# Two state-space layers on one core: the old sum added on VectorE at the copy-out, and u * D made by ScalarE

## The chip, the cores and the metric

The kernel runs on one core of a Trainium2 chip. The metric is the device time of one execution in microseconds; three runs of the kernel before are at hand. In the text, PE is TensorE's matrix unit and PEld its loading of weights, DVE is VectorE, ACT is ScalarE, POOL is GpSimd, and SP is SyncE, whose queue issues nearly all DMAs. PSUM is the memory that TensorE writes, SBUF the memory that everything else works in.

## The reference

Four images of 64 x 64 positions with 192 channels pass through two layers, each added to its own input. Cut to what matters, with D_INNER = 384 channels and 16 states:

```python
# layer 0: four directions k over the 4096 positions, each with its own weights
h = dA * h + dBu                       # 16 states per channel, along the positions
y_k = einsum("bkdn,bkn->bkd", h, ct)   # sum over the states
out_k = y_k + u * Ds                   # skip term
y = out_0 + flip(out_2) + transpose(out_1) + transpose(flip(out_3))
# then LayerNorm over the channels, times silu(z), and a projection back to 192

# layer 1: the same four directions over a 3 x 3 depthwise convolution,
# all with the same weights
xc = silu(conv(x_val) + conv_b)
y = y1 + y2 + y3 + y4                  # each one: scan(u) + u * D_param
```

The skip term of the second layer is the same for all four directions, so their sum is 4 * D * u.

## The kernel before

**First layer.** `FirstLayer.run` goes through the four images (batches) one after the other: `between` finishes one batch and projects the next, then `scans` does the recurrences. The sum y lives in DRAM as 4096 x 384. `project_steps` writes u times the sum of the D's into it, and every piece of scan adds to it.

`scans` cuts a batch into 32 items. An item is one direction k and one chunk c of 512 positions; directions 0 and 2 (by row) come first, then 1 and 3 (by column), 16 items each. Every item has 16 states, and one state is one step of the loop over g; n is the state's number in its item. For each state, ACT makes the decays (`decay`, L728) and the product with B (`b_product`, L716), PE turns the product from positions on partitions to channels on partitions (`turn_x`, L733), DVE scans three blocks of 128 channels (`scan`, L741, with a small reduction L751 that keeps the last column), POOL multiplies by C (`c_product`, L755), and PE turns the result back while it adds it into three PSUM banks (`add_y`, L768). The additions lag by LAG = 3 states. At state 3 there are therefore none; at state 4 those of two states are done, and later one state per step.

The order on PE, DVE, ACT and POOL is written out by hand: each engine executes its instructions in the order in which the loop emits them. `Item.steps` lists the preparation of the next items with their places (dt through `dt_rows` L632, `absolute` L638 on ACT, `delta` L661 on DVE and so on), and `prepare` puts them into the loop. The DMAs on SP are ordered by a scheduler and wait in their queue for buffers; those of the C rows (`bct`, L721, one for two states, three buffers) wait for POOL.

Old y enters an item in PSUM: `load` brings the chunk of y to SBUF as `yold` (L601, one buffer), `start_y` (L762) multiplies the identity by it on PE at states 3 and 4 with the flag that opens the accumulation, and `add_y` adds on top. When the item is complete, `end_y` (L781) copies the banks to SBUF on DVE during states 2 and 3 of the next item, and a DMA (L784) stores them. The load for the next item is issued at state 5, except where the direction changes from row to column: there the chunk of y is spread over all that was stored before, and the load comes after the last `end_y` of the item before:

```python
if n == 5 and i + 1 < len(items) and items[i + 1].k % 2 == it.k % 2:
    q = items[i + 1]
    q.yold = load("yold", self.y_dram, q.k, q.c)
```

**Second layer.** `SecondLayer.project` goes through the four batches. For each of three channel blocks e, ACT writes the padded image (`pad`, L1123), and for each half q of the image ACT starts the convolution with tap 0 (`acc`, L1135) and DVE adds the eight others (L1137). ACT makes u from it with Silu (L1138), copies the border rows and columns that the scans need (L1145, L1148), and PE multiplies each block of 128 positions of u by `dg`, a diagonal matrix with 4 * D, which turns it and scales it at once (L1155). ACT copies the result out (L1159) and SP stores it as the first content of y. `acc` and `u` have three buffers each, `dq` two banks. The order of this stage is set by a scheduler. `prepare`, `scans` and `finish` follow.

Of the kernel before, what the change touches and what calls it, by code (L numbers as in the profile page):

```python
# [10 lines left out]
F32 = mybir.dt.float32  # L11
AF = mybir.ActivationFunctionType
# [4 lines left out]
DI, NS, DR, KD = 384, 16, 12, 4  # L17
ND = DI // 128
CB, NC2 = 96, 2
LC = 512  # L20
# [382 lines left out]
class FirstLayer:  # L403
# [168 lines left out]
    def scans(self):  # L572
        nc, tc = self.tc.nc, self.tc
        with ExitStack() as ctx:
# [3 lines left out]
            ps_y = pool("psy", 1, space=bass.MemoryType.PSUM)  # L578
            ps_x = pool("psx", 3, space=bass.MemoryType.PSUM)
            ps_m = pool("psm", 2, space=bass.MemoryType.PSUM)  # L580
            ident = self.ident
# [16 lines left out]
            def load(name, dram, k, c):  # L598
                t = p1.tile([128, NJ, DI], F32, name=name)
                for to, of in rows(t, dram, k, c):  # L600
                    nc.sync.dma_start(to, of)  # L601
                return t
# [100 lines left out]
            items = []  # L703
# [4 lines left out]
            flat = [(it, n) for it in items for n in range(NS)]  # L708
# [45 lines left out]
                it, n = flat[g]  # L754
                nc.gpsimd.tensor_tensor(hs[g], hs[g], bc(cs[g - n % 2][:, n % 2, :], 1, ND), ALU.mult)  # L755

            def start_y(it, b):

                if b == 0:
                    it.yp = [ps_y.tile([128, LC], F32, name=f"yp{i}") for i in range(ND)]  # L760
                yo = it.yold.rearrange("p j e -> p (j e)")[:, b * LC : (b + 1) * LC]
                nc.tensor.matmul(it.yp[b], ident, yo, start=True, stop=False, skip_group_check=True)  # L762

            def add_y(g, b):
                it, n = flat[g]
                for i in range(NJ):
                    j, d = divmod(b * NJ + i, ND)
                    nc.tensor.matmul(  # L768
                        it.yp[b][:, i * 128 : (i + 1) * 128],
                        hs[g][:, d, j * 128 : (j + 1) * 128],  # L770
                        ident,
                        start=False,
                        stop=n == NS - 1,
                        is_transpose=True,
                        skip_group_check=True,
                    )

            def end_y(it, b):
                if b == 0:
                    it.yt = p1.tile([128, NJ, DI], F32, name="yt")  # L780
                nc.vector.tensor_copy(it.yt.rearrange("p j e -> p (j e)")[:, b * LC : (b + 1) * LC], it.yp[b])  # L781
                if b == ND - 1:
                    for of, to in rows(it.yt, self.y_dram, it.k, it.c):
                        nc.sync.dma_start(to, of)  # L784
# [3 lines left out]
            def gate_in(t, e):  # L788
                zs[t, e] = self.in_proj(ps_m.tile([128, LC], F32, name="zp", tag="m"), ND + e, t)
# [8 lines left out]
            with tc.manual_schedule(engines={nc.tensor.engine, nc.scalar.engine, nc.vector.engine, nc.gpsimd.engine}):  # L798
                tc.keep_in_program_order(nc.scalar.preload_act_table_set("natural_log_exp_and_others"))
                plan = {}  # L800
                for i, it in enumerate(items):
                    for ahead, n, engine, f in it.steps():
                        if i < ahead:
                            f()
                        else:
                            plan.setdefault((i - ahead) * NS + n, []).append((engine, f))
                for t in range(NCH):
                    for e in range(ND):
                        plan.setdefault(t * NS + 13 + e, []).append(("pe", lambda t=t, e=e: gate_in(t, e)))
                        plan.setdefault(t * NS + 15 + e, []).append(("act", lambda t=t, e=e: gate_out(t, e)))  # L810

                def prepare(g, engine):
                    for e, f in plan.get(g, []):
                        if e == engine:
                            f()

                items[0].yold = load("yold", self.y_dram, items[0].k, items[0].c)
                c_rows(0)
                b_product(0)
                b_product(1)  # L820
                decay(0)
                for d in range(ND):
                    turn_x(0, d)
                LAG = 3
                late = []
                for g in range(N + LAG + 1):
                    i, n = divmod(g, NS)
                    it = items[i] if g < N else None
                    before = items[i - 1] if i > 0 else None
                    prepare(g, "act")  # L830
                    if g + 2 < N:
                        if g % 2 == 0:
                            c_rows(g + 2)
                        b_product(g + 2)
                    if g + 1 < N:
                        decay(g + 1)
                    adds = [[] for _ in range(ND)]
                    if it is not None:
                        for at, b in (((LAG, 1), 0), ((LAG, 2), 1), ((LAG + 1, 0), 2)):
                            if at[0] == n:  # L840
                                adds[at[1]].append((start_y, it, b))

                    ready = [x for x in late if x <= g - LAG and (n > LAG or x // NS < i)][:2]
                    for j, (x, b) in enumerate((x, b) for x in ready for b in range(ND)):
                        adds[j // len(ready)].append((add_y, x, b))
                    late = [x for x in late if x not in ready]
                    for d in range(ND):
                        if g < N:
                            scan(g, d)
                        if d == 1:  # L850
                            prepare(g, "dve")
                        if before is not None and (n, d) in ((LAG - 1, 2), (LAG, 0), (LAG, 1)):
                            end_y(before, {2: 0, 0: 1, 1: 2}[d])
                            if (n, d) == (LAG, 1) and it is not None and it.yold is None:
                                it.yold = load("yold", self.y_dram, it.k, it.c)
                        if g + 1 < N:
                            turn_x(g + 1, d)
                        for f, *a in adds[d]:
                            f(*a)
                    if g < N:  # L860
                        prepare(g, "pe")
                        c_product(g)
                        late.append(g)
                        prepare(g, "pool")
                        if n == 5 and i + 1 < len(items) and items[i + 1].k % 2 == it.k % 2:
                            q = items[i + 1]
                            q.yold = load("yold", self.y_dram, q.k, q.c)


    def finish(self, batches):  # L870
# [152 lines left out]
class SecondLayer(FirstLayer):  # L1023
# [6 lines left out]
    def __init__(self, tc, ctx, consts, w, dram, alive):  # L1030
        nc = tc.nc
        self.tc, self.w, self.alive, self.dram = tc, w, alive, dram
        self.ident, self.group, self.one = consts
        wp = ctx.enter_context(tc.tile_pool(name="ws", bufs=1))
# [30 lines left out]
        nc.vector.memset(self.keep, 1.0)  # L1065
        for at in (0, SEG, 3 * SEG - 1, 4 * SEG - 1):
            nc.vector.memset(self.keep[:, at : at + 1], 0.0)

        self.dg = wp.tile([128, ND, 128], F32, name="dg_s")
        d = load("D", [128, 1, ND])  # L1070
        nc.vector.tensor_scalar_mul(d, d, float(KD))
        for e in range(ND):
            nc.vector.tensor_scalar_mul(self.dg[:, e, :], self.ident, d[:, 0, e : e + 1])

    def run(self, batches):

# [11 lines left out]
    def project(self, batches):  # L1088
        nc, tc = self.tc.nc, self.tc
        with ExitStack() as ctx:  # L1090
# [17 lines left out]
            for b, (_, y, gate, uc_dram) in enumerate(batches):  # L1108
# [7 lines left out]
                for e in range(ND):  # L1116
# [12 lines left out]
                    for q in range(2):  # L1129
                        nh = half * rows  # L1130
                        acc = pa.tile([128, nh, HW], F32, name="acc")
                        part = lambda tap: pad[:, q * nh + tap // 3 : q * nh + tap // 3 + nh, tap % 3 : tap % 3 + HW]
                        weight = lambda tap: self.cw[:, e, tap : tap + 1]
                        u = pu.tile([128, nh, HW], F32, name="u")
# [6 lines left out]
                        n = SEG // HW  # L1141
# [5 lines left out]
                                to = uc[:, r, e, k * SEG : (k + 1) * SEG].rearrange("p (w h) -> p w h", h=HW)  # L1147
                                nc.scalar.copy(to[:, :, q * nh : (q + 1) * nh], wide[:, col : col + n, :])  # L1148

                        flat = u.rearrange("p h w -> p (h w)")  # L1150
                        for t in range(half):
                            dq = pq.tile([128, NJ, 128], F32, name="dq")
                            for j in range(NJ):
                                at = t * LC + j * 128
                                nc.tensor.matmul(  # L1155
                                    dq[:, j, :], flat[:, at : at + 128], self.dg[:, e, :], start=True, stop=True
                                )
                            du = pl.tile([128, NJ, 128], F32, name="du")
                            nc.scalar.copy(du, dq)  # L1159
                            at = (q * half + t) * LC  # L1160
                            to = y[at : at + LC, e * 128 : (e + 1) * 128].rearrange("(j p) e -> p j e", p=128)
                            nc.sync.dma_start(to, du)
# [470 lines left out]
```

## Time and profile before

| what | us |
|---|---|
| median of 3 runs | 11105.2 |
| lowest and highest run | 11085.83 and 11113.26 |
| the profiled execution | 11106.54 |
| its span, first to last instruction | 11104.6 |
| PE busy in the span | 9551.9 (86%) |
| DVE busy | 9693.3 (87%) |
| ACT busy | 9775.8 (88%) |
| POOL busy | 8587.9 (77%) |

The first layer takes the first 9670 us or so, the second the rest: its projection lies roughly between 9750 and 10330 us. The granted TensorE clock is 0.939 of full speed over the span, and the trace has it in stretches of full and of half speed. A busy share is a mean over stages with different limits, so the question for each part of the change is which wait ends last in its own stage. The profile counts one f32 matmul of this kind as two records and one f32 transpose as one, so "x768" for L762 is 384 matmuls, three for each of the 128 items.

### The profile page before, as it was taken

Reading aid. Unit: us, or ns where it says so; the run is one execution under the profiler, and the core shown is the slowest. Engines: PE = TensorE matmul, PEld = TensorE weight load, DVE = VectorE, ACT = ScalarE, POOL = GpSimd, SP = SyncE. Lnnn points to the kernel's source line nnn. Section 1 sums busy time; section 2 is a strip of 40 time slices with the busy share of each in tenths; the row PEclk is TensorE's granted clock in tenths of the full one; section 3 lists DMA queues with packets and bytes.
Section 4 is the critical chain, followed back from the end, with each engine's and each line's share of the span. In section 5 each row is a group of like instructions: output and inputs, shape, how many; then the busy total and the mean of one; then the engine's idle time right before and its main releaser. Section 6 shows DMA issues by size and latency. Waiting matters only on the chain. (4 is left out here: it accounts for less than half of the span.)

```text
span 11104.6 us, 172135 instructions
## 1 busy us (share of the span) xinstructions
PE 9551.9 (86%) x61449; PEld 7273.6 (66%) x61449; DVE 9693.3 (87%) x11515; ACT 9775.8 (88%) x16979; POOL 8587.9 (77%) x2776
## 2 busy tenths in 40 slices
PE   7998888888988888888988888889988888788677
PEld 4776666666776666656776666657766766655366
DVE  4999899976999899968999899949998999878675
ACT  5999999977999999969999999959999999856477
POOL 3999899955999899938999899929998999700370
PEclk8999999998999999998999999989999999989688
DMA  4333344344333344443333433353333434433458
GB/s 125 109 108 101 91 101 101 98 137 127 109 106 101 92 101 99 98 159 112 109 103 96 98 97 99 93 168 109 109 99 95 98 98 98 120 119 123 157 131 272
DMA packets 833671, 1267.54 MB, mean 114 GB/s; under 512 B 102026, under 2 KB 517655, under 8 KB 832292
## 3 DMA queue, kind: packets, MB, share of 16 engines
q1 hardware_dynamic: 827940, 1250.15, 40.5%
q0 software_dynamic: 4864, 6.29, 0.4%
q8 instruction: 488, 8.00, 0.3%
q14 instruction: 379, 3.10, 0.1%
HBM read 955.83 MB, written 300.42 MB: 113 GB/s over the span
## 5 line engine op out<-in xcount | busy, mean ns | idle before, releaser
L755 POOL TENSOR_TENSOR h<-h,bct 128x1536 f32<-128x1536 f32 x2048 | 7062.9, 3470 | 579.9 <-DVE carry L751 477.5
L741 DVE TENSOR_TENSOR_SCAN h<-a,carry,x 128x512 f32<-128x512 f32 x5376 | 6604.9, 1266 | 231.0 <-PE x L733 194.9
L733 PE MATMUL x<-ident,xT 128*128 128x128 f32 x24576 | 4000.8, 287 | 811.8 <-DVE h L741 710.1
L716 ACT ACTIVATE xT<-dtuT,bT 128x384 f32<-128x384 f32 x8192 | 4358.8, 609 | 93.0 <-PE x L733 87.3
L733 PEld LDWEIGHTS x<-ident,xT 128*128 128x128 f32 x24576 | 2804.0, 145 | 2136.5 <-DVE h L741 920.5
L728 ACT ACTIVATE a<-dt,A_log_f 128x512 f32<-128x512 f32 x6144 | 3977.7, 716 | 0.0
L768 PE MATMUL yp<-ident,h 128*128 128x128 f32 x24576 | 3703.1, 277 | 9.2 <-POOL h L755 9.2
L768 PEld LDWEIGHTS yp<-ident,h 128*128 128x128 f32 x24576 | 2944.2, 144 | 78.8 <-issue 62.6
L632 PE MATMUL dp<-xd,w_dtb_f 13*128 13x512 f32 x1536 | 882.7, 657 | 216.0 <-DVE dt L661 211.3
L741 DVE TENSOR_TENSOR_SCAN h<-a,x 128x512 f32<-128x512 f32 x768 | 899.1, 1207 | 191.3 <-PE x L733 114.0
L645 POOL TENSOR_SCALAR wl<-e 128x1536 f32<-128x1536 f32 x128 | 189.2, 1478 | 799.3 <-ACT e L641 406.2
L519 PE MATMUL pp<-xT,w_in 96*128 96x512 f32 x1152 | 539.2, 617 | 1.1 <-DVE xw L562 1.1
L632 PEld LDWEIGHTS dp<-xd,w_dtb_f 13*128 13x128 f32 x1536 | 235.0, 189 | 456.6 <-DVE dt L661 341.3
L762 PE MATMUL yp<-yold,ident 128*128 128x512 f32 x768 | 445.1, 664 | 72.7 <-DMA yold<-y 72.7
L1137 DVE SCALAR_TENSOR_TENSOR acc<-pad,conv_w_s,acc 128x2048 f32<-128x2048 f32 x192 | 439.3, 2342 | 53.5 <-ACT acc L1135 52.9
L638 ACT ACTIVATE e<-dp 128x512 f32<-128x512 f32 x384 | 224.7, 585 | 269.3 <-DVE dt L661 155.4
L1118 POOL MEMSET pad<- 128x66 f32 x12 | 1.9, 158 | 578.4 <-DVE acc L1137 458.9
L658 POOL TENSOR_TENSOR e<-e,wl 128x1536 f32<-128x1536 f32 x128 | 445.1, 3477 | 0.3
L655 POOL TENSOR_TENSOR e<-e,dt 128x1536 f32<-128x1536 f32 x128 | 442.9, 3460 | 0.3
L751 DVE TENSOR_REDUCE carry<-h 128x3 f32<-128x3 f32 x2048 | 322.7, 158 | 70.4
L519 PEld LDWEIGHTS pp<-xT,w_in 96*128 96x128 f32 x1152 | 221.3, 198 | 244.4 <-issue 234.3
L661 DVE SCALAR_TENSOR_TENSOR dt<-dp,e 128x512 f32<-128x512 f32 x384 | 255.5, 666 | 65.2 <-POOL e L658 58.7
(170 smaller groups left out, 6875.3 us busy)
## 6 DMA issues: line engine op xcount, KB each, us to landing
bct<-xp SPq DMA_DIRECT2D x1024, 512.0 KB, 4.9
uT<-uT SPq DMA_DIRECT2D x64, 768.0 KB, 4.7
yold<-y SPq DMA_DIRECT2D x64, 768.0 KB, 7.9
y<-yt SPq DMA_DIRECT2D x64, 768.0 KB, 4.5
uT<-uT SPq DMA_DIRECT2D x128, 384.0 KB, 5.0
yold<-y SPq DMA_DIRECT2D x128, 384.0 KB, 5.3
y<-yt SPq DMA_DIRECT2D x128, 384.0 KB, 4.6
zg<-gate SPq DMA_DIRECT2D x64, 768.0 KB, 6.3
```

The source lines that it names most:

```text
L519: self.tc.nc.tensor.matmul(pp, self.w_in[:, i, e * 128 : (e + 1) * 128], self.xT[:, i, t * LC : (t + 1) * LC], start=(i == 0), stop=(i == ...
L632: nc.tensor.matmul(self.dp[d], w, self.xd[0 : DR + 1, :], start=True, stop=True)
L655: nc.gpsimd.tensor_tensor(self.e, self.e, self.dt, ALU.subtract)
L658: nc.gpsimd.tensor_tensor(self.e, self.e, self.wl, ALU.add)
L716: nc.scalar.mul(xTs[g][:, j, :], it.dtuT[:, j * DI : (j + 1) * DI], it.bT[:, j, n : n + 1])
L728: nc.scalar.activation(as_[g][:, d, :], it.dt[:, d, :], AF.Exp, scale=scale)
L733: nc.tensor.transpose(xs[g, d][:, j * 128 : (j + 1) * 128], xTs[g][:, j, d * 128 : (d + 1) * 128], ident)
L741: nc.vector.tensor_tensor_scan(along(hs[g][:, d, :], it.k), along(as_[g][:, d, :], it.k), along(xs.pop((g, d)), it.k), 0.0 if it.first els ...
L755: nc.gpsimd.tensor_tensor(hs[g], hs[g], bc(cs[g - n % 2][:, n % 2, :], 1, ND), ALU.mult)
L762: nc.tensor.matmul(it.yp[b], ident, yo, start=True, stop=False, skip_group_check=True)
L768: nc.tensor.matmul(it.yp[b][:, i * 128 : (i + 1) * 128], hs[g][:, d, j * 128 : (j + 1) * 128], ident, start=False, stop=n == NS - 1, is_tr ...
L1137: nc.vector.scalar_tensor_tensor(acc, part(tap), weight(tap), acc, ALU.mult, ALU.add)
```

## The change

In the first layer, `start_y` goes. The first addition of an item opens each bank (`start` at n == 0 and i == 0), and `end_y` adds old y on DVE while it copies from PSUM. Every item now loads its own `yold` at state 8, the turn of directions included. In the second layer ACT writes 4 * D * u over `acc` in one instruction for each half image, with D as the scale per partition, and PE turns it with a plain transpose. The matrix `dg` is no longer built.

```diff
-            def start_y(it, b):
-
-                if b == 0:
-                    it.yp = [ps_y.tile([128, LC], F32, name=f"yp{i}") for i in range(ND)]
-                yo = it.yold.rearrange("p j e -> p (j e)")[:, b * LC : (b + 1) * LC]
-                nc.tensor.matmul(it.yp[b], ident, yo, start=True, stop=False, skip_group_check=True)
-
             def add_y(g, b):
                 it, n = flat[g]
+                if n == 0 and b == 0:
+                    it.yp = [ps_y.tile([128, LC], F32, name=f"yp{i}") for i in range(ND)]
                 for i in range(NJ):
...
-                        start=False,
+                        start=n == 0 and i == 0,
...
             def end_y(it, b):
                 if b == 0:
                     it.yt = p1.tile([128, NJ, DI], F32, name="yt")
-                nc.vector.tensor_copy(it.yt.rearrange("p j e -> p (j e)")[:, b * LC : (b + 1) * LC], it.yp[b])
+                part = slice(b * LC, (b + 1) * LC)
+                yt, yo = (t.rearrange("p j e -> p (j e)")[:, part] for t in (it.yt, it.yold))
+                nc.vector.tensor_add(yt, it.yp[b], yo)
...
-                items[0].yold = load("yold", self.y_dram, items[0].k, items[0].c)
...
-                    if it is not None:
-                        for at, b in (((LAG, 1), 0), ((LAG, 2), 1), ((LAG + 1, 0), 2)):
-                            if at[0] == n:
-                                adds[at[1]].append((start_y, it, b))
...
-                            if (n, d) == (LAG, 1) and it is not None and it.yold is None:
-                                it.yold = load("yold", self.y_dram, it.k, it.c)
...
-                        if n == 5 and i + 1 < len(items) and items[i + 1].k % 2 == it.k % 2:
-                            q = items[i + 1]
-                            q.yold = load("yold", self.y_dram, q.k, q.c)
+                        if n == 8:
+                            it.yold = load("yold", self.y_dram, it.k, it.c)
...
-        self.dg = wp.tile([128, ND, 128], F32, name="dg_s")
         d = load("D", [128, 1, ND])
-        nc.vector.tensor_scalar_mul(d, d, float(KD))
-        for e in range(ND):
-            nc.vector.tensor_scalar_mul(self.dg[:, e, :], self.ident, d[:, 0, e : e + 1])
+        self.d4 = wp.tile([128, ND], F32, name="d4_s")
+        nc.vector.tensor_scalar_mul(self.d4, d[:, 0, :], float(KD))
...
-                        flat = u.rearrange("p h w -> p (h w)")
+                        nc.scalar.activation(acc, u, AF.Identity, scale=self.d4[:, e : e + 1])
+                        flat = acc.rearrange("p h w -> p (h w)")
...
-                                nc.tensor.matmul(
-                                    dq[:, j, :], flat[:, at : at + 128], self.dg[:, e, :], start=True, stop=True
-                                )
+                                nc.tensor.transpose(dq[:, j, :], flat[:, at : at + 128], self.ident)
```

## The prediction

> **What bounds the kernel now.** I read the page first, for what is busy. These are its rows of the first layer's scans; a row gives busy time and mean ns of one instruction, then idle time just before it and what ended most of that.
>
> ```profile
> L755 POOL TENSOR_TENSOR h<-h,bct 128x1536 f32<-128x1536 f32 x2048 | 7062.9, 3470 | 579.9 <-DVE carry L751 477.5
> L741 DVE TENSOR_TENSOR_SCAN h<-a,carry,x 128x512 f32<-128x512 f32 x5376 | 6604.9, 1266 | 231.0 <-PE x L733 194.9
> L716 ACT ACTIVATE xT<-dtuT,bT 128x384 f32<-128x384 f32 x8192 | 4358.8, 609 | 93.0 <-PE x L733 87.3
> L762 PE MATMUL yp<-yold,ident 128*128 128x512 f32 x768 | 445.1, 664 | 72.7 <-DMA yold<-y 72.7
> ```
>
> The scans of one batch last about 2195 us (first to last L751), four times. In the stretch 700 to 1100 us ACT is busy 389.2 of 400 us, DVE 382.9, POOL 375.7, PE 352.3. Three engines are nearly full, and PE, from which the change takes most, is the loosest. So the 445 us of L762 are not 445 us of time; what counts is where PE makes the others wait. The view of waits names one such place:
>
> ```profile
> PE yp L762 <- DMA yold<-y: 72.7, 4, 18.4
> ```
>
> Four waits of 18 us, one per batch. The timeline at 1316 us (start, length, idle before) shows that everything stands still there:
>
> ```profile
> 1317.03 2.07 PE L762 MATMUL yp<-yold,ident 128*128 128x512 f32 x2 [18.07 <-DMA yold<-y]
> ...
> 1320.05 2.13 ACT L716 ACTIVATE xT<-dtuT,bT 128x384 f32<-128x384 f32 x4 [15.95 <-PE x L733]
> 1320.06 1.22 DVE L741 TENSOR_TENSOR_SCAN h<-a,x 128x512 f32<-128x512 f32 x1 [17.70 <-PE x L733]
> ...
> 1321.61 3.45 POOL L755 TENSOR_TENSOR h<-h,bct 128x1536 f32<-128x1536 f32 x1 [14.62 <-ACT xT L716]
> ```
>
> This is item 17 of 32, the first of the column direction. Its load of old y must wait until the item before has stored, and start_y on PE waits for the load, with turn_x for DVE queued behind. From the ends of L751 (one per state) I took the length of each item: most lie between 67.1 and 71.4 us, item 17 of the four batches is 86.2, 84.8, 84.7 and 84.9.
>
> Splitting DVE's idle time by state: from state 12 of one item to state 8 of the next it waits for almost nothing (0.03 us a state, 0.2 us at states 3 and 5). Its waits are at states 9 to 11, when ACT has itself stood 1.4 us at Abs (L638) for DVE's delta. So in a common item neither the matmuls of L762 nor their place hold anybody, and their removal gives little directly.
>
> One exception is PE's clock. At state 3 nothing is to be added to y, and PE has only the turns and start_y. In stretches of 3.4 us around 1726 us (busy time and count of PE, PEld, DVE, ACT, POOL, then PEclk):
>
> ```profile
> 1722.40:1725.80 3.40, 1.24 (x11) 0.82 (x9) 3.40 (x5) 3.40 (x7) 3.40 (x2) 1.00 0.22 72
> 1725.80:1729.20 3.40, 3.40 (x11) 2.04 (x10) 3.37 (x5) 3.40 (x7) 3.40 (x2) 0.50 0.89 197
> 1729.20:1732.60 3.40, 3.40 (x22) 2.38 (x21) 3.10 (x4) 3.40 (x7) 3.40 (x2) 1.00 0.40 119
> ```
>
> A stretch with 1.24 us of PE work is followed by one at half clock. There start_y takes longer and pushes a turn back, and DVE waits (timeline):
>
> ```profile
> 1726.14 1.91 PE L762 MATMUL yp<-yold,ident 128*128 128x512 f32 x2
> ...
> 1732.00 0.60 PE L733 MATMUL x<-ident,xT 128*128 128x128 f32 x4
> ...
> 1732.70 2.59 DVE L741 TENSOR_TENSOR_SCAN h<-a,carry,x 128x512 f32<-128x512 f32 x2 [0.38 <-PE x L733]
> ```
>
> The clock in the trace halves in this way from state 3 in 34 of 128 items. There state 5 takes 4.39 us instead of 3.77, and in the first eight items of a batch state 3 takes 0.6 us more too.
>
> [...]
>
> **The change, part by part.** The groups for the replaced operations:
>
> ```profile
> L681 DVE TENSOR_TENSOR dtuT<-tp,uT 128x512 f32<-128x512 f32 x384 | 259.0, 674 | 18.8 <-PE tp L675 8.7
> L781 DVE COPY yt<-yp 128x512 f32<-128x512 f32 x384 | 258.2, 674 | 17.7 <-PE yp L768 17.4 <-issue 0.3
> L1155 PE MATMUL dq<-dg_s,u 128*128 128x128 f32 x768 | 115.1, 315 | 52.0 <-ACT u L1138 50.7 <-ACT du L1159 1.3
> L1135 ACT ACTIVATE acc<-pad,conv_w_s 128x2048 f32<-128x2048 f32 x24 | 48.3, 2013 | 0.6
> ```
>
> 1. end_y: 384 copies from PSUM become 384 adds of PSUM and SBUF. L681 is that shape, under the same load: 674 ns against 674. Cost 0.
>
> 2. Turn of direction: the load is issued at state 8 of its own item and first used ten states (some 40 us) later, in end_y. The store it must wait for was issued at state 3. SP still waits for that store's landing (4.6 us) ahead of the load's issue, as before, with bct loads queued behind it; POOL has two pairs of states in hand (14 us), so nobody is reached. Item 17 falls from 85.2 (mean) to 68.3: 16.9 x 4 = **-68**. The usual loads also lose SP's wait for PE (186.9 us in SP's view of waits), on no path: SP waits 6953 us for POOL anyway.
>
> 3. L762 gone, 384 matmuls of 1.16 us on PE. Directly: DVE's 34 slips at state 5 go, 34 x 0.62 = 21, and some 0.6 x 8 at state 3: **-26**.
>
> 4. The gap at state 3. Without start_y, PE has some 6.5 us with only 16 turns (12 in 5.3 us), so each item holds a window like the one at 1722.4, wherever it falls. Half clock then reaches into state 4, where PE has 24 additions and 12 turns to do, 4.0 us at full clock (0.44 us for four) and 7.8 at half (0.87), against DVE's 3.77. By hand, in that order (turn, 8 adds, three times): half clock for the first 3.2 us makes DVE wait 0; for 4.3 us 0.5; for 6 us 1.2. How far it reaches depends on the window's phase and on whether the second window is also too empty (it would hold 8 to 15 turns and adds; windows below about 12 are followed by half clock nearly always in this trace, fuller ones seldom). Over the phases I get 0.4 us an item; bounds 0 (a start before state 4) and 1.3 (two full windows). Take 0.4 x 124 = **+50**.
>
> 5. Second layer: 24 more ACTIVATEs at 2.01 us, 48 us on ACT, which from 9900 to 10340 us is busy 59%, beside the convolution (L1137) that DVE runs without gaps, 192 x 2.34. acc is now held until turned, some 8 us longer; its next writer is needed two convolutions (37 us) later, so that cover holds. In the order after, tap 0 comes behind the new ACTIVATE and up to three du copies, still well inside. It counts where batches meet and at the end (DVE idles 14 us between batches): +2.0, and the turns save: 16 matmuls go from two passes to one, some 2 us at each. Four places of 0 to 1: **+2**, between -6 and +10. The removed setup of dg is 0.7 us beside other work. DMA count and bytes do not change.
>
> Sum: -68 - 26 + 50 + 2 = -42. The profiled execution took 11106.5 (span 11104.6), 1.3 above the median of 11105.2; so **11064**.
>
> **Rivals.** A: half clock costs nothing, as start_y's own 1.9 us was what hurt. For it: the shown item slips because of start_y. Against: windows get emptier. 11064 - 50 = 11014. B, slower: the gap makes two half-clock windows in each item; at 1.3 us, 161 - 94 + 2 = +69, 11174. It decides from 1.0 us per item, where the sum is 33 above the present time. For it: PE is already full at states 4 to 8. C: the stall at item 17 moves, say to end_y because the load in two pieces queues badly: +68 on the sum, 11132. Against: ten states of slack. D: the 48 us of ACT in the second layer come on the path, 11110; against, 41% idle. E: the steady gain of 2 and 3 only in part, as ACT's 97% takes over: that lies in my range.
>
> **How the numbers follow.** Chances: the sum above 0.58 (own range 11026 to 11113, for 0.1 to 0.8 us an item), A 0.17, B 0.10, C 0.08, D 0.07. A difference of 0.3%, 33 us, is about what a measurement of this kernel tells from none. Faster by more: A, and two thirds of the first case: 0.57. Within: the rest of it, D and half of C: 0.30. Slower: B and part of C: 0.13. The range 11005 to 11125 leaves out B, much of C and the edge of A.
>
> **What would show it.** Right: no wait at item 17 (all items 67 to 71 us); end_y's add at 670 to 680 ns; PEclk of 0.5 from state 3 in nearly every item, and state 5 longer by some 0.4; second layer's projection unchanged within 10 us. Wrong: state 5 at 3.77 in all items (A) or above 4.8 (B), a wait of end_y for yold (C), or DVE gaps between convolutions (D).

## The result, and the profile after

The changed kernel took **11067.1 us** (median of 15 runs, 11053.0 to 11079.5), the kernel before 11101.3 beside it (15 runs, 11084.4 to 11113.4). The ratio is 0.9971, with a 95% interval of 0.9964 to 0.9978: faster by about 0.3%, 34 us. The profiled execution took 11062.1 (span 11060.3), 44.4 less than that of before; the granted clock of TensorE over the span went from 0.939 to 0.918.

The groups of the scans after; the columns are those of before. The additions into yp now stand at L763, end_y at L778.

```profile
L755 POOL TENSOR_TENSOR h<-h,bct 128x1536 f32<-128x1536 f32 x2048 | 7066.0, 3473 | 550.0 <-DVE carry L751 508.2
L741 DVE TENSOR_TENSOR_SCAN h<-a,carry,x 128x512 f32<-128x512 f32 x5376 | 6615.6, 1267 | 274.7 <-PE x L733 224.1
...
L716 ACT ACTIVATE xT<-dtuT,bT 128x384 f32<-128x384 f32 x8192 | 4358.2, 609 | 34.7 <-PE x L733 29.7
...
L763 PE MATMUL yp<-ident,h 128*128 128x128 f32 x24576 | 3839.9, 285 | 9.2 <-POOL h L755 9.2
```

Before, the additions stood so:

```profile
L768 PE MATMUL yp<-ident,h 128*128 128x128 f32 x24576 | 3703.1, 277 | 9.2 <-POOL h L755 9.2
```

POOL, DVE and ACT do the same work at the same price; the additions, the same in number and shape, have become dearer for PE. DVE's idle time ahead of these scans has grown from 231.0 to 274.7 us, 224.1 of it waiting for turned products (L733), while ACT's idle time ahead of its products has fallen from 93.0 to 34.7: one wait has gone and another has grown. The row of the multiplications by the identity has gone, and the view of waits has no line of PE waiting for yold.

The operations that the change put in, and the taps of the convolution beside them:

```profile
L1123 DVE SCALAR_TENSOR_TENSOR acc<-pad,conv_w_s,acc 128x2048 f32<-128x2048 f32 x192 | 440.6, 2342 | 46.2 <-ACT acc L1121 44.9
...
L778 DVE TENSOR_TENSOR yt<-yp,yold 128x512 f32<-128x512 f32 x384 | 258.4, 674 | 20.9 <-PE yp L763 17.4 <-issue 0.7
...
L1142 PE MATMUL dq<-ident,acc 128*128 128x128 f32 x384 | 64.6, 323 | 68.2 <-ACT acc L1136 64.1 <-ACT du L1144 3.9
...
L1136 ACT ACTIVATE acc<-u,d_s 128x2048 f32<-128x2048 f32 x24 | 48.2, 2009 | 0.0
```

The taps before:

```profile
L1137 DVE SCALAR_TENSOR_TENSOR acc<-pad,conv_w_s,acc 128x2048 f32<-128x2048 f32 x192 | 439.3, 2342 | 53.5 <-ACT acc L1135 52.9
```

end_y's add takes 674 ns like the copy that it replaces, and its waits are for PE's last additions (17.4 us, four times, where batches end); none is for the load of old y. The transposes of the second layer are 384 records instead of 768, 64.6 us instead of 115.1; the new ACTIVATE L1136 takes 2009 ns, 24 times; DVE's wait before the taps has fallen from 52.9 to 44.9 us.

From the ends of the small reduction L751 I took the length of every item and state. Item 17 of the four batches is now 65.6, 66.0, 66.2 and 65.6 us (before 86.2, 84.8, 84.7, 84.9): 77 us gone. The rest of the first layer, up to the last of these reductions, has become longer by some 45, so that this comes at 9630.3 instead of 9662.4 us. Where this comes from is seen in stretches of one window of the clock each, 3.41 us in this trace (columns: busy time and count of PE, PEld, DVE, ACT, POOL, then PEclk):

```profile
1506.62:1510.03 3.41, 1.26 (x8) 0.84 (x8) 3.41 (x5) 3.41 (x8) 3.41 (x2) 1.00 0.24 85
1510.03:1513.44 3.41, 2.07 (x9) 1.70 (x10) 3.38 (x4) 3.41 (x7) 3.41 (x2) 0.50 0.81 218
1513.44:1516.86 3.42, 3.42 (x18) 3.42 (x17) 3.31 (x5) 3.42 (x7) 3.42 (x2) 0.50 0.29 86
```

The first, in state 3, holds 1.26 us of PE work. The next two run at half clock (0.50). The first of these two holds no more than nine instructions, eight turns and the start of the additions; the last section counts what follows on such windows. The timeline of the same item (start, length, work, and in brackets the idle time before) shows what comes of it:

```profile
1513.36 1.91 PE L763 MATMUL yp<-ident,h 128*128 128x128 f32 x8
...
1515.07 1.06 PE L733 MATMUL x<-ident,xT 128*128 128x128 f32 x4
...
1515.92 1.50 PE L763 MATMUL yp<-ident,h 128*128 128x128 f32 x8
...
1517.26 0.60 PE L733 MATMUL x<-ident,xT 128*128 128x128 f32 x4
...
1517.96 1.28 DVE L741 TENSOR_TENSOR_SCAN h<-a,carry,x 128x512 f32<-128x512 f32 x1 [0.45 <-PE x L733]
```

Eight additions take 1.91 and 1.50 us, where at full clock they take 1.04 (the same trace at 1653.94 us); the third turn that state 5 needs (the one at 1517.26) comes 0.45 us too late, and DVE, which hardly idles otherwise here, stands for it. In the 128 items half clock starts 125 times from state 3 or 4, against 37 before.

### The profile page after: what moved, and what is told of

The parts are those of the page before. It is cut to its first block, busy times and chain, and to the rows that moved or that the text cites. A ratio compares the mean times of both kernels' runs of the same rounds, so it can differ in the third digit from the quotient of the medians.

```text
span 11060.3 us, 169780 instructions
## 1 busy us (share of the span) xinstructions
PE 9381.9 (85%) x60297; PEld 7300.4 (66%) x60297; DVE 9708.2 (88%) x11512; ACT 9816.8 (89%) x17003; POOL 8590.8 (78%) x2776
## 5 line engine op out<-in xcount | busy, mean ns | idle before, releaser
L741 DVE TENSOR_TENSOR_SCAN h<-a,carry,x 128x512 f32<-128x512 f32 x5376 | 6615.6, 1267 | 274.7 <-PE x L733 224.1
L733 PE MATMUL x<-ident,xT 128*128 128x128 f32 x24576 | 4118.0, 293 | 982.4 <-DVE h L741 881.1
L716 ACT ACTIVATE xT<-dtuT,bT 128x384 f32<-128x384 f32 x8192 | 4358.2, 609 | 34.7 <-PE x L733 29.7
L733 PEld LDWEIGHTS x<-ident,xT 128*128 128x128 f32 x24576 | 2888.9, 148 | 2170.3 <-DVE h L741 1013.3
L763 PE MATMUL yp<-ident,h 128*128 128x128 f32 x24576 | 3839.9, 285 | 9.2 <-POOL h L755 9.2
L763 PEld LDWEIGHTS yp<-ident,h 128*128 128x128 f32 x24576 | 3079.1, 149 | 11.1 <-POOL h L755 11.1
L632 PE MATMUL dp<-xd,w_dtb_f 13*128 13x512 f32 x1536 | 881.8, 657 | 201.5 <-DVE dt L661 198.4
L632 PEld LDWEIGHTS dp<-xd,w_dtb_f 13*128 13x128 f32 x1536 | 232.4, 187 | 441.7 <-DVE dt L661 327.7
L1123 DVE SCALAR_TENSOR_TENSOR acc<-pad,conv_w_s,acc 128x2048 f32<-128x2048 f32 x192 | 440.6, 2342 | 46.2 <-ACT acc L1121 44.9
L751 DVE TENSOR_REDUCE carry<-h 128x3 f32<-128x3 f32 x2048 | 322.8, 158 | 70.4
L931 PE MATMUL op<-w_out,v 128*128 128x192 f32 x1536 | 292.1, 340 | 10.1 <-DVE v L921 7.1
```

The costliest lines, as they stand in the source:

```text
L632: nc.tensor.matmul(self.dp[d], w, self.xd[0 : DR + 1, :], start=True, stop=True)
L716: nc.scalar.mul(xTs[g][:, j, :], it.dtuT[:, j * DI : (j + 1) * DI], it.bT[:, j, n : n + 1])
L733: nc.tensor.transpose(xs[g, d][:, j * 128 : (j + 1) * 128], xTs[g][:, j, d * 128 : (d + 1) * 128], ident)
L741: nc.vector.tensor_tensor_scan(along(hs[g][:, d, :], it.k), along(as_[g][:, d, :], it.k), along(xs.pop((g, d)), it.k), 0.0 if it.first els ...
L751: nc.vector.tensor_reduce(kept, last(hs[g], it.k), mybir.AxisListType.X, ALU.max)
L763: nc.tensor.matmul(it.yp[b][:, i * 128 : (i + 1) * 128], hs[g][:, d, j * 128 : (j + 1) * 128], ident, start=n == 0 and i == 0, stop=n == N ...
```

## The experiments

The medians of the kernel before beside them were 11103.5, 11101.1 and 11101.3 us in the three groups of runs (e1 to e4, e5 to e7, e8 and e9). "Item" in this table is the mean of 112 items (without the first, second, 17th and 32nd of each batch), "17" the mean of the four items 17; the columns of states are the same mean in us, and the last two count the starts of half clock from states 3 or 4, and from 8 to 10, in all 128 items.

| kernel | median us | state 3 | state 5 | 9 | 10 | 11 | item | 17 | half 3-4 | half 8-10 |
|---|---|---|---|---|---|---|---|---|---|---|
| before | 11101.3 | 5.64 | 3.96 | 5.02 | 4.83 | 4.87 | 68.41 | 85.2 | 37 | 93 |
| changed | 11067.1 | 5.70 | 4.20 | 5.06 | 4.82 | 4.99 | 68.87 | 65.9 | 125 | 94 |
| e2 | 11070.9 | 5.69 | 4.16 | 5.04 | 4.86 | 4.99 | 68.86 | 65.8 | 125 | 98 |
| e3 | 11026.8 | 5.65 | 3.94 | 4.96 | 4.89 | 4.91 | 68.46 | 65.7 | 39 | 91 |
| e4 | 11031.8 | 5.71 | 3.76 | 5.53 | 4.67 | 4.72 | 68.51 | 67.8 | 0 | 102 |
| e7 | 11027.1 | 5.71 | 3.77 | 5.34 | 4.71 | 4.73 | 68.38 | 67.6 | 20 | 106 |
| e5 | 10977.0 | 5.72 | 3.76 | 5.29 | 4.43 | 4.62 | 67.95 | 66.6 | 2 | 55 |
| e6 | 10933.6 | 5.75 | 3.76 | 5.06 | 4.29 | 4.62 | 67.59 | 66.6 | 4 | 8 |
| e9 | 10928.5 | 5.75 | 3.76 | 5.03 | 4.29 | 4.62 | 67.57 | 65.9 | 36 | 4 |
| e8 | 11004.3 | 5.71 | 3.76 | 5.08 | 4.29 | 4.62 | 67.57 | 85.5 | 8 | 11 |

The theory after the result was the prediction's own: the turn of direction gives some 77 us, and the clock takes about half of it back. The rival was that something else takes it back: the load at state 8, the add, or ACT's new work in the second layer.

**e1 and e2, one part of the change each.** e1 is the kernel before with the second layer's part alone:

```diff
+                        nc.scalar.activation(acc, u, AF.Identity, scale=self.d4[:, e : e + 1])
+                        flat = acc.rearrange("p h w -> p (h w)")
...
+                                nc.tensor.transpose(dq[:, j, :], flat[:, at : at + 128], self.ident)
```

> The kernel before with the second layer's part alone: 4 * D * u made by ScalarE and turned. Theory (the prediction's sum, step 5): the 48 us of new ScalarE work lie beside the convolution on DVE, so the time is that before within 10 us, about 11100, and DVE idles no more between the convolutions. Rival (the second layer gives a share of the gain, since the projection came out some 5 us shorter in the trace after): 11085 to 11095. Rival D (ScalarE on the path): 11148.

Measured: 11099.3 us, ratio 0.9995 (0.9986 to 1.0003). No difference can be told. The convolution took 519.0 us from the first to the last tap, 523.4 in the profile of before; but e4, which has this part of the change too, took 526.2, and e8, which does not, 518.8, so that these few us say nothing of the change.

e2 has the first layer's part alone: `start_y` gone, the load at state 8, the add in `end_y`:

```diff
-                nc.vector.tensor_copy(it.yt.rearrange("p j e -> p (j e)")[:, b * LC : (b + 1) * LC], it.yp[b])
+                nc.vector.tensor_add(yt, it.yp[b], yo)
...
+                        if n == 8:
+                            it.yold = load("yold", self.y_dram, it.k, it.c)
```

> The kernel before with the first layer's part alone: old y added on DVE, its load at state 8. Theory: it carries the whole difference, so 11065 to 11072; item 17 is as short as the others, half clock starts in state 3 or 4 of nearly every item, and the other items are some 0.4 us longer than before. Rival (half of the gain is the second layer's): 11085.

Measured: 11070.9, ratio 0.9970 (0.9958 to 0.9982), the whole effect, with the same items and the same 125 starts of half clock as the changed kernel. What remains to be explained lies in the first layer.

**e3, the stall taken away without the rest.** The kernel before with its multiplications by the identity; only the four items at the turn of direction load other data, which are there in time:

```diff
                             q.yold = load("yold", self.y_dram, q.k, q.c)
+                        elif n == 5 and i + 1 < len(items):
+                            q = items[i + 1]
+                            q.yold = load("yold", uT_dram, q.k, q.c)
```

> The kernel before, start_y and its matmuls kept, but item 17 loads its first content from another DRAM tensor (uT) that nobody writes at that time, one item ahead, so that it need not wait; old y of these 4 items is left out of the sum. Theory: the wait at the turn of direction is worth 68 to 76 us by itself, so about 11030, which is below the changed kernel, as here start_y still fills state 3 and the other items stay as before. Rival (the gain of the change comes from PE's lighter load or from DVE's order, and the wait is hidden otherwise): no faster than 11075.

Measured: 11026.8, ratio 0.9932 (0.9918 to 0.9945). The stall alone is worth 77 us (11103.5 - 11026.8), and this kernel, which keeps the 384 multiplications, is 40 us **faster** than the changed one. So something else in the first layer's part costs time: that the multiplications are gone from PE, or the add and the load that came in their place. e4 tells these apart. Half clock starts 39 times from state 3, much as in the kernel before.

**e4, useless work in the gap.** The changed kernel, with 24 turns of the identity into yp in state 3, eight after each turn_x; the first addition of the item overwrites them:

```diff
+            def fill_open(it, d, m):
+                if d == 0:
+                    it.yp = [ps_y.tile([128, LC], F32, name=f"yp{i}") for i in range(ND)]
+                for i in range(m):
+                    nc.tensor.matmul(
+                        it.yp[0][:, :128], ident, ident, start=True, stop=True, is_transpose=True, skip_group_check=True
+                    )
...
+                        if it is not None and n == LAG:
+                            fill_open(it, d, 8)
```

> The changed kernel with 24 useless transposes of the identity on PE in state 3 of every item (8 after each turn, into a bank that the first addition opens anew). Theory: the time lost in the common items is PE's half clock after an empty state 3, so more work on PE makes it faster: half clock from states 3 to 5 nearly gone, state 5 at 3.77 us, 124 items shorter by 0.4 to 0.6 us, together 50 to 75 us, so 10995 to 11020. Rival (the common items are longer for the adds on DVE, the loads at state 8, or PE's load): the same time as the changed kernel or slower, 11067 to 11100.

Measured: 11031.8, ratio 0.9934 (0.9920 to 0.9948): 35 us faster than the changed kernel for 3072 instructions more on PE. Half clock starts nowhere from states 3 or 4, and state 5 is 3.76 in the mean. So the add and the load, which e4 keeps, are not what cost the time. The gain is smaller than expected (10995 to 11020), and the table says where the rest went: half clock now starts 47 times from state 8 (13 in the changed kernel), and state 9 rose from 5.06 to 5.53.

**e7, fewer of them.** As e4 with 3 instead of 8 after each turn_x, nine in an item.

> The changed kernel with 9 useless turns in state 3 instead of the 24 of e4_fill3. Theory (a window needs some 12 to 15 instructions of TensorE to keep the next one at full clock; in state 3 and 4 the changed kernel has fewer than 12): with 9 more, most windows are filled; half clock starts from states 3 and 4 in at most a third of the items, against 125 of 128 in the changed kernel and none with 24, and the time lies between 11025 and 11050. Rival (the gain of e4_fill3 comes from something else than the clock, such as the order in which the turns put the other instructions): the time stays with e4_fill3, 11032, or with the changed kernel, 11067, whatever the number of half clock starts.

Measured: 11027.1, ratio 0.9936 (0.9922 to 0.9949). Half clock still starts 20 times from state 3, but state 5 is at 3.77: 16 of the 20 are over within the first 2.1 us of state 4, where the additions begin at 1.8 (the median), and so hardly reach them. The dose of 9 does as much as that of 24. By its time alone e7 does not part the theory from its rival, since both allow about 11030; for the clock speak the lengths of the additions above and e8 below.

**e5 and e6, the other half-clock windows.** From states 8 to 10 half clock starts over 90 times in all the kernels so far. Two kernels add turns of a zero tile, accumulated into yp, ahead of the rows of dt: e5 has 6 in state 7 and 6 in state 8, e6 10 and 4, both beside e4's 24.

```diff
+            def fill_zero(it, m):
+                for i in range(m):
+                    nc.tensor.matmul(
+                        it.yp[0][:32, :128], zero, ident, start=False, stop=False, is_transpose=True, skip_group_check=True
+                    )
...
+                            if not filled and f in late_rows:
+                                fill_zero(items[g // NS], FILL[g % NS])
+                                filled = True
```

> The changed kernel with 24 turns of the identity into yp, useless, in state 3 of each item (as in e4_fill3), and beside them 6 turns of a zero tile in state 7 and 6 in state 8, which add nothing to yp. Theory (TensorE's clock is halved for a window after one with too few of its instructions, and that is what states 8 to 10 still pay): the half clock starts from state 8 fall from 47 items to under 15, state 9 comes down from above 6 us in those items to under 5.2, and the time falls from 11032 to between 10900 and 11000. Rival (states 7 and 8 are full for VectorE, so that turns put ahead of the rows of dt only delay what VectorE waits for): each of the 12 turns costs its 0.11 us in the state where it stands, up to 1.3 us for an item, and the time is 11030 to 11190.

> As e5_fill3_78, with 10 turns of the zero tile in state 7 and 4 in state 8. Theory: the window that is too empty lies over the end of state 7 and the start of state 8, so it is filled as well or better: half clock starts from states 8 to 10 in fewer items than in e5_fill3_78, time 10880 to 11000. Rival (delay): 14 turns of 0.11 us, up to 1.5 us for an item: 11030 to 11220.

e5 measured 10977.0, ratio 0.9885 (0.9870 to 0.9900): inside the theory's range, but its counts failed: half clock starts 37 times from state 8, not under 15, and in these items state 9 takes 5.95 us in the mean, not under 5.2. e6, with more of them in state 7, measured **10933.6**, ratio 0.9848 (0.9835 to 0.9862), with 8 starts of half clock from states 8 to 10, and state 9 back at 5.06: the delay of the rival did not come. The stretch from 700 to 1100 us in the changed kernel and then in e6 (columns as above):

```profile
700.00:1100.00 400.00, 345.52 (x2415) 278.69 (x2413) 382.91 (x435) 388.51 (x687) 375.43 (x118) 0.95 0.38 100
```

```profile
700.00:1100.00 400.00, 362.18 (x2682) 292.27 (x2681) 387.60 (x439) 393.54 (x697) 381.74 (x119) 1.00 0.38 104
```

PE is busier, 362.2 us instead of 345.5, its clock is at 1.00, and DVE, ACT and POOL each do 1 to 2% more in the same time. The groups of e6, in which L777 and L783 are the useless turns, L763 the additions and L634 the rows of dt:

```profile
L743 DVE TENSOR_TENSOR_SCAN h<-a,carry,x 128x512 f32<-128x512 f32 x5376 | 6588.5, 1266 | 156.3 <-PE x L735 135.2 <-ACT a L730 9.8 <-POOL h L757 4.1
...
L763 PE MATMUL yp<-ident,h 128*128 128x128 f32 x24576 | 3625.8, 273 | 9.3 <-POOL h L757 9.3
...
L634 PE MATMUL dp<-xd,w_dtb_f 13*128 13x512 f32 x1536 | 879.6, 655 | 105.9 <-DVE dt L663 102.9 <-ACT e L640 2.1 <-DVE dtuT L683 1.0
...
L777 PE MATMUL yp<-ident 128*128 128x128 f32 x3072 | 407.0, 276 | 0.0
...
L783 PE MATMUL yp<-ident,zero 128*32 128x128 f32 x1680 | 225.1, 274 | 0.0
```

In the changed kernel the row of dt reads:

```profile
L632 PE MATMUL dp<-xd,w_dtb_f 13*128 13x512 f32 x1536 | 881.8, 657 | 201.5 <-DVE dt L661 198.4 <-ACT e L638 2.1 <-DVE dtuT L681 1.0
```

632 us of useless turns (407.0 + 225.1) shorten the additions from 3839.9 to 3625.8, DVE's idle time ahead of its scans from 274.7 to 156.3, and PE's idle time ahead of the rows of dt, nearly all of it a wait for DVE's delta, from 201.5 to 105.9.

**e8, both kernels near full clock.** The kernel before, multiplications and stall included, with 9 turns in state 3 and e6's 10 and 4:

```diff
+                        if it is not None and n == LAG:
+                            fill_open(it, d, 9)
```

Here `fill_open` makes its turns only for d = 0, ahead of the first `start_y`.

> The kernel before, with the identity still multiplied by old y, and with useless turns that keep TensorE's windows full: 9 in state 3, ahead of the first of these multiplications, and 10 and 4 turns of the zero tile in states 7 and 8 as in e6_fill3_78b. Set beside e6_fill3_78b (10934), it is the first layer's change with the clock taken out on both sides. Theory (without the clock, all that the change brings is the stall at the turn of direction, 77 us): 70 to 90 us above e6_fill3_78b, 11004 to 11024, all of it in item 17 of each batch; the other items as long as there, 67.3 in the mean. Rival 1 (the removed multiplications also held somebody in other items by the time that they take): above e6_fill3_78b by over 100 us, 11034 or more, with the other items longer by 0.2 us or more. Rival 2 (what the turns in states 7 and 8 gain needs the room that the change makes, so the kernel before gains nothing from them): 11080 to 11110.

Measured: 11004.3, ratio 0.9913 (0.9899 to 0.9926), 70.7 above e6 and 75.8 above e9. The stall is there, and hardly any half clock:

```profile
PE yp L762 <- DMA yold<-y: 72.4, 4, 18.3
```

```profile
700.00:1100.00 400.00, 365.24 (x2620) 288.20 (x2617) 386.69 (x439) 392.60 (x696) 380.72 (x119) 0.99 0.38 102
```

Its common item is as long as that of e6 and e9, 67.57 against 67.59 and 67.57. So both rivals fell: with the clock kept up on both sides, the first layer's change is worth its stall and nothing else that can be told.

**e9, the two doses together:** 9 turns in state 3, 10 and 4 in states 7 and 8.

> The changed kernel with the turns of the zero tile as in e6_fill3_78b (10 and 4 in states 7 and 8) and 9 instead of 24 useless turns in state 3 as in e7_fill3_few. Theory (9 are enough for the windows of states 3 and 4, and the 15 others only take TensorE's time): within 15 us of e6_fill3_78b, 10920 to 10945, half clock starts in fewer than 30 of 128 items. Rival (without the 24 some windows of state 3 stay too empty, and shift the half clock into the full states): half clock starts in more than 40 items and 10950 to 10990.

Measured: **10928.5**, ratio 0.9843 (0.9829 to 0.9856), the lowest of all, though not told apart from e6. The time is as the theory had it; the count is not (40 starts, 36 of them from state 3, where under 30 were expected), and as in e7 those in state 3 cost nothing. Both kernels of the comparison are beaten, by 173 and 139 us.

## Why the prediction was right

The sum was -42, and the profiled executions differ by 44.4, the medians by 34. Its terms were less exact than their sum.

**Step 1, the add in end_y, 0: right.** 674 ns before and after, beside a POOL that is busy 375 of 400 us.

**Step 2, the turn of direction, -68: right in mechanism, 9 us too small.** Measured -77 (85.2 to 65.9 in the mean, four times), and e3 shows that the stall alone gives it. The mis-sized term is the 68.3 that I took for a common item: the first item of a direction has no carried state to take in, and its scans are shorter. The timeline after, at the end of item 16 and the start of item 17:

```profile
1287.56 3.62 DVE L741 TENSOR_TENSOR_SCAN h<-a,carry,x 128x512 f32<-128x512 f32 x3
...
1291.32 3.44 DVE L741 TENSOR_TENSOR_SCAN h<-a,x 128x512 f32<-128x512 f32 x3
```

Three scans take 3.44 instead of 3.62 us, in 16 states 2.9 us. SP issued the loads of old y from state 5 of their item on, sooner than the place in the loop that I reckoned from; they landed in at most 9.7 us, and no end_y waited for one, so rival C fell.

**Steps 3 and 4, -26 and +50, so +24: right in mechanism, 21 us too small.** The common items became longer by 0.46 us, 51 us in 112 of them; the rest of the layer became shorter by some 6, nearly all of it between the batches, where this part of the change does nothing: +45. Among the 112 is item 18, the first of the other column direction, which has no carried state either: it fell from 68.3 to 66.1, so that the other 108 lost 0.55 each. State 5, on which both steps rested, came out as worked: above the 3.76 that it takes at full clock stood 0.20 us an item before (22 us in 112; 21 forecast for the 34 slips), and 0.44 after (0.4 forecast), +26 net. What the sum did not have is the rest. The 5 us at state 3 did not come back (5.64 to 5.70, +6), and states 9 and 11 became longer by 0.04 and 0.12 (+5 and +13): I priced half clock only where the change makes the gap, though the kernel had 93 starts of it at states 8 to 10 too. That those starts cost time is shown by e6, where 8 of them are left and states 10 and 11 fall to 4.29 and 4.62. State 9 stays at 5.06 there, with 14 turns put in ahead of it, and state 3 at 5.75, so that for these two the clock is not shown to be the cause. Why state 11 costs more after the change, with as many starts as before, no run here settles.

Rival A, that half clock costs nothing, fell with e3 and e4. Rival B needed 1.0 us an item; 0.46 was measured. Rival E, that ACT takes over part of the gain, did not hold at state 5, which e4 has at 3.76; at state 3, where nothing came back, it stays open.

**Step 5, the second layer, +2:** e1 tells no difference from 0. From the end of the first layer to the end of the span the profiled executions differ by 12 us, 5 of them in the convolution and most of the others in the preparation, scans and finish behind it, which the change does not touch. e4 and e6, which have the change in the second layer, take 1446 and 1445 us for this stretch, the kernel before 1442 and the changed one 1430, so I read nothing from the 12. Rival D fell: DVE's gaps before the taps shrank.

So the gain of the turn was 9 us larger than in the sum and the loss in the rest of the layer 21 larger, and behind the first layer the profiled executions differ by 14 more than forecast, where e1 shows no effect. That these nearly cancelled is luck. Without that last part the difference is about that of the medians, 34 us, 8 less than the sum. The clock's whole cost was larger than the step said. An estimate from the common item of e8, which has little half clock left: it took (68.41 - 67.57) x 112 = 94 us from the kernel before, and (68.87 - 67.57) x 112 = 146 from the changed one.

## What to carry to other kernels

Work taken off an engine with room to spare gained something here only where that engine had made somebody wait: at one load in four places, 72.7 us in the view of waits, and not by the 445 us of matmuls. Before thinning out TensorE's instructions in a full pipeline, look at PEclk in stretches of one window of its clock, 3.41 us here: in the trace after, each of the 166 windows that were left with fewer than 12 turns or additions, and nothing else, was followed by one at half clock, and DVE, which is full, paid for it (state 5 at 4.20 us in the mean instead of 3.76). Where that happens, some useless turns in the gap can be worth more than the change: 9 in state 3 and 14 in states 7 and 8 made the kernel 139 us faster here, the change alone 34.

## What the runs showed of the hardware

In the stretches around 1510 us, a window of the clock with 1.26 us of work in 3.41 was followed by half clock, and one with nine instructions at half clock, 2.07 us, by a second such window. In both traces the clock changes only on a grid of 3.41 us (382 stretches of one clock before, 542 after). Of its windows inside the scans that hold turns and additions alone, or nothing, so many were followed by one at half clock:

| instructions on PE in the window | before | after |
|---|---|---|
| fewer than 12 | 48 of 48 | 166 of 166 |
| 12 to 15 | 5 of 37 | 37 of 134 |
| 16 or more | 0 of 1188 | 0 of 1230 |

Of the 48 before, 17 hold nothing; they lie in the four stalls at the turn of direction. Of those in the trace after that ran at full clock themselves, all 125 with less than 1.6 us of PE work were followed by half clock, and none of the 1137 with 1.6 or more. Busy time does not decide by itself, though: of the full-clock windows that also hold rows of dt (L632, 13 x 512), 62 of 74 with 2.0 to 2.5 us of PE work were followed by half clock, which is where most of the starts at states 8 to 10 come from. Why half clock follows these windows at more PE work than the others, no run here settles.

Useless turns were enough to keep the clock up here: in e4, where everything added in state 3 was a turn, half clock started from states 3 or 4 in none of the 128 items, against 125 times in the changed kernel, and with the 14 turns of e6 as well the clock from 700 to 1100 us was 1.00, against 0.95. I had not expected that a busier TensorE (362.2 of these 400 us in e6, 345.5 in the changed kernel) could go with a kernel 133 us faster.
